# Forming the last outputs of a Strassen-tiled attention layer from sums in PSUM, and reordering the last query projection, scores and output products

## The chip, the core and the metric

The kernel runs on one core of a Trainium2 chip. The metric is device time in microseconds (us): the median of several runs of the whole program. The engines named below are TensorE (PE: matmuls into PSUM), VectorE (DVE: elementwise work), ScalarE (ACT: copies and exponentials), GpSimd (POOL: here it only issues weight loads) and SyncE (SP: here it only issues DMAs).

## The reference

The input `x` is eight sequences of 256 tokens with 512 features. It is normalised to `xn`. Attention with 32 query heads of 128 features and 8 key/value heads (four query heads share one) gives `s`; a gated mixture of small experts gives a factor `g`; the result is `x + s * silu(g)`.

```python
q = (hidden_states @ wq.T).reshape(bsz, q_len, H, HD).transpose(0, 2, 1, 3)
...
scores = scores * scale                       # per-key factors
scores = scores + causal
probs = jax.nn.softmax(scores.astype(jnp.float32), axis=-1).astype(dt)
attn = jnp.einsum('bhqk,bhkd->bhqd', probs, v)
attn = attn.transpose(0, 2, 1, 3).reshape(bsz, q_len, H * HD)
return attn @ wo.T
...
x = x + s * g
```

All data are 32-bit floats.

## The kernel before

**Tiling.** The sequences are worked on in four blocks of two (`tb` 0 to 3; 512 tokens each). Each block has eight groups (`g` 0 to 7), one for each key/value head with its four query heads. A step is one (block, group) pair, 32 in all. A unit is one sequence of one step, so each step has two. A tile name ends in these numbers: unit 7_0 is group 7, first sequence.

**Matrix products.** Every large product (query, key, value and output projection) is cut into 2 x 2 blocks and done with seven block products in place of eight, after Strassen and Winograd. In a query projection (`quad`, line 486) the seven products go to three PSUM banks, `pa`, `pd` and `pe`. Bank `pa` takes four of them one on top of the other; between two of them ScalarE copies the bank aside (`p1`, `u2`, `u3`), and VectorE adds `pd` or `pe` to such a copy to give `cq`. In an output projection (`out_project`, line 841) each of the seven products gets its own bank `po`, and VectorE adds it to one of seven running sums in SBUF, `acc_1` to `acc_7`, which collect over the eight groups. Its left operands are four blocks `a` (the attention outputs, copied from PSUM by ScalarE) and three VectorE sums of them, `s_4` to `s_6`, plus one difference written over an `a`.

**The end of a block.** After group 7, `finish` (line 917) combines `acc_1` to `acc_7` into the four output quarters with seven more additions, and for each quarter multiplies by the stored gate (`g`, half of it), adds `x` (`xf`) and stores it: `result`, line 953.

**A softmax unit** (`softmax`, line 681) has three pieces on TensorE, score rows (7,6), (5,4,3) and (2,1,0) into two rotating PSUM banks `sc`. VectorE scales, masks and takes minima (`z`, `least`). ScalarE takes exponentials into `p`, a single buffer that all units share. VectorE multiplies by the reciprocal sums (`total`) and transposes `p` in 32 x 32 blocks into `blocks`, again a single buffer. SyncE writes `blocks` to DRAM with four DMAs (`there`) and reads it back with one (`pT`). Then `values` (line 806) multiplies it by the value rows (`av`), two pieces for each unit, and ScalarE copies `av` to `a`.

**What sets the order.** TensorE's order is written out by hand: the loop at line 1165 collects the pieces of each step (`sa`, `sb`: scores of the two units; `va`, `vb`: values of the units two back; `oa`, `ob`: output products of the step before and of this one) and lays them down, woven with the next step's query projection (`main`). Step 30 is group 6 of the last block and holds the last query projection; steps 31 to 33 have no projection left to weave. All other engines are ordered by a planner (`Plan.run`, line 195): each job has a due time, derived from the TensorE pieces that need its result, and the planner emits the ready job that is due first. Every engine then runs its queue strictly in that order. Weights for the output products come through a ring of eight buffers (`wo`), for the projections through a ring of nine (`w`); POOL issues a load as soon as the buffer's last reader is done.

In the profile every instruction carries line 118, since all are issued through the `InOrder` helper there; groups are told apart by tile names.

Of the kernel before, what the change touches and what calls it, by code (L numbers as in the profile page):

```python
# [44 lines left out]
P = 128  # L45
# [8 lines left out]
NB = 2  # L54
# [202 lines left out]
def layer(ctx: ExitStack, tc: tile.TileContext, x, wquad, woquad, raT, bT, table, out):  # L257
# [583 lines left out]
    def out_project(tb, g):  # L841
# [19 lines left out]
        for i, (to, a, b, op) in enumerate(Features.steps):  # L861
            a_done[to] = add(
                "dve", 0.61, lambda i=i: sum_up(i),
                after=[a_done[a], a_done[b]] + Features.before(i, a_done),
                opens=[ah[to]] if to != S3 else [], closes=[ah[a], ah[b]],
            )
        pieces = {}

        def product(k, a, w):
# [41 lines left out]
            for i in Outputs.sums:  # L911
                sums_of["wo", g, i].near = (pieces[1], 0.0)
        if g == KV - 1:
            finish(tb)
        return [pieces[k] for k in (1, 2, 6, 5, 7, 4, 3)]

    def finish(tb):
        M = {k: acc[tb, k] for k in range(1, 8)}

        def put(to, a, b, closes=()):  # L920
# [11 lines left out]

        def inputs(b):
            box = {}

            pl, tag = (two, "c") if b and tb == NTB - 1 else (x_pool, "x")
            xh, gh = hold(tag), hold(tag)
            rows = x[bass.ds(tb * TB + b * S, S), :].rearrange("(t p) o -> p t o", p=P)

            def load(what):  # L940
                box[what] = pl.tile([P, 2, D], F32, tag=tag, name=f"{what}{tb}_{b}")
                src = rows if what == "xf" else gates_dram[tb][:, bass.ts(b, 2), :]
                nc.sync.dma_start(out=box[what], in_=src)

            near = (M[2]["last"], -12.0)
            done = [
                add("sp", 0.3, lambda: load("g"), after=gates[tb][2 * b : 2 * b + 2], opens=[xh],
                    near=near, lag=9.0),
                add("sp", 0.3, lambda: load("xf"), opens=[gh], near=near, lag=9.0),
            ]  # L950
            loads[b] = box, [xh, gh], done
# [197 lines left out]
    cleared = add("pool", 2.0, clear)  # L1149

    LAG_V = 2
    held = []

    def part(make, u):
        return make(*units[u]) if 0 <= u < len(units) else []
# [9 lines left out]
    for n in range(len(steps) + 2):  # L1165
        last = n >= len(steps)
        tb, g = (NTB, 0) if last else steps[n]
        (sa, va), (sb, vb) = (
            (part(softmax, u), part(values, u - LAG_V)) for u in (NB * n, NB * n + 1)
        )  # L1170
        ob = out_project(*steps[n - 1]) if 0 < n <= len(steps) else []
        oa, held = held, ob[2:]
        fill = oa[:1] + va[:1] + sa[:1] + oa[1:2] + va[1:] + sa[1:2] + oa[2:4] + sa[2:]
        later = [oa[4:], ob[:1], vb[:1], sb[:1], ob[1:2], vb[1:], sb[1:2], sb[2:]]
        if not last:
            if g == 1 and tb:
                route, turn, silus[tb] = experts(tb)
                fill += route
                later.append(turn)
            at = g if tb == 0 else g - 2  # L1180
            if 0 <= at < NT:
                fill += silus[tb][at]
            if tb + 1 < NTB and g == KV - 2:
                turns = norm(tb + 1)
                for t in range(NT):
                    later[t] = later[t] + [turns[t]]
        later = [piece for some in later for piece in some]
        if n == len(steps) - 1:

            fill, later = sa + sb, oa + va + vb + ob[:2]  # L1190
        main = []
        for q in quads[n + 1] if not last else []:
            main += make_quad(*q)
        if not main:
            lay(fill + later)
        elif len(main) > 7:
            lay(woven(main, fill + later, 0.9))
        else:
            lay(woven(main, fill, 1.0) + later)
# [30 lines left out]
```

## Time and profile before

| what | value |
|---|---|
| median of 3 runs | 1370.39 us (1365.43 to 1372.58) |
| the profiled execution, its own time | 1371.18 us |
| its span, first to last instruction | 1369.4 us |
| TensorE busy | 1334.2 us, 97% |
| VectorE busy | 1096.7 us, 80% |
| ScalarE busy | 618.0 us, 45% |
| mean granted TensorE clock | 0.995 |

A line of the page or of the timeline gives a start (us from the span's start), a duration, the engine, the operation and `output<-inputs`, with how many instructions were merged (`x8`: a 32-bit matmul is two records, so one block product of four matmuls is x8). In square brackets stands the time for which the engine sat idle just before, and what released it. In a table of stretches, each row gives the length of the stretch, then the busy time of each engine in it, the granted TensorE clock, the busy share of the DMA engines and the GB/s moved. The chain of waits is followed back from the last instruction: at each moment it names the work, or the transfer, that the end depended on.

### The profile page before, as it was taken

To read this page: it belongs to the slowest core of one execution; us is meant where nothing else is said; L and a number is where in the kernel's file an instruction comes from. 1 tells how busy PE (TensorE), PEld (TensorE's weight loads), DVE (VectorE), ACT (ScalarE), POOL (GpSimd) and SP (SyncE) were. 2 spreads that over 40 slices of the span, in tenths; PEclk is the share of its full clock that TensorE was granted. 3 is DMA by queue.
4 is the path that set the end of the run, shared out by engine and by line. 5 is a ranking of instruction groups with operands and counts; after the bars stand their busy time and mean duration, and the time that the engine had idled before them with its cause. 6 is when DMAs were issued, how large, how long until landed. Compare 5 with 4: busy or idle time off the path is not lost.

```text
span 1369.4 us, 19896 instructions
## 1 busy us (share of the span) xinstructions
PE 1334.2 (97%) x6512; PEld 1171.1 (86%) x6512; DVE 1096.7 (80%) x2822; ACT 618.0 (45%) x1587; POOL 314.4 (23%) x579
## 2 busy tenths in 40 slices
PE   7999999999999999999999999999999999999986
PEld 6888888888888888888888788888888888888865
DVE  5899989897978759598688776869877878777886
ACT  3465453453534535354434444345543354434430
POOL 2322232222221122222222112222123121221110
PEclk9999999999999999999999999999999999999998
DMA  5578676766766665766766756676667576575563
GB/s 173 187 248 257 204 212 201 233 204 199 236 192 211 200 215 173 218 209 187 219 187 197 217 183 194 190 231 201 173 211 213 168 247 191 179 220 169 185 205 117
DMA packets 106134, 275.81 MB, mean 201 GB/s; under 512 B 15984, under 2 KB 52848, under 8 KB 106032
## 3 DMA queue, kind: packets, MB, share of 16 engines
q0 software_dynamic: 45760, 149.98, 35.5%
q1 hardware_dynamic: 59520, 123.76, 29.2%
q8 instruction: 53, 0.87, 0.3%
q10 hardware_dynamic: 752, 0.80, 0.2%
q14 instruction: 49, 0.40, 0.1%
HBM read 194.79 MB, written 79.69 MB: 200 GB/s over the span
## 4 chain that ended last, share of the span: by engine, by line
PE 83%; DVE 8%; DMA 7%; issue 1%; SPq 0%; ACT 0%; DVEq 0%
PE po L118 24%; PE paq L118 14%; PE av L118 11%; PE sc L118 9%; PE pdq L118 7%; DMA pT<-there 5%; PE pak L118 4%; PE peq L118 3%; PE pav L118 3%; PE pdk L118 2%; DMA there<-blocks 2%; PE pdv L118 1%; DVE blocks L118 1%; PE dle L118 1%; DVE acc L118 1%; PE lme L118 1%
## 5 line engine op out<-in xcount | busy, mean ns | idle before, releaser
L118 ACT ACTIVATE p<-z,least 128x256 f32<-128x256 f32 (+7 forms) x512 | 207.7, 407 | 192.3 <-DVE least L118 138.4
L118 PE MATMUL po<-wo,a 128*128 128x256 f32 x1024 | 241.6, 379 | 1.4 <-ACT a L118 1.4
L118 PEld LDWEIGHTS po<-wo,a 128*128 128x128 f32 x1024 | 192.2, 190 | 25.7 <-ACT a L118 2.2
L118 PE MATMUL av<-pT,v 128*128 128x256 f32 x768 | 186.9, 382 | 10.4 <-DMA pT<-there 10.4
L118 DVE CUSTOM_DVE_ANT_0 z<-sc,tab 128x256 f32<-128x256 f32 (+7 forms) x512 | 134.0, 300 | 68.2 <-PE sc L118 64.8
L118 PE MATMUL po<-wo,s 128*128 128x256 f32 x768 | 183.8, 383 | 3.5 <-DVE s L118 2.7
L118 PE MATMUL paq<-XT,w 128*128 128x256 f32 x768 | 182.0, 380 | 0.3 <-ACT u3q L118 0.3
L118 PEld LDWEIGHTS av<-pT,v 128*128 128x128 f32 x768 | 145.3, 191 | 32.7 <-issue 7.5
L118 PEld LDWEIGHTS sc<-kk,qTq 128*128 128x128 f32 x1024 | 159.3, 191 | 13.4 <-issue 0.8
L118 PE MATMUL sc<-kk,qTq 128*128 128x256 f32 (+7 forms) x1024 | 168.9, 303 | 0.3 <-DVE least L118 0.2
L118 PEld LDWEIGHTS po<-wo,s 128*128 128x128 f32 x768 | 144.7, 191 | 28.2 <-issue 6.3
L118 DVE TENSOR_TENSOR acc<-acc,po 128x512 f32<-128x512 f32 x196 | 132.7, 678 | 41.5 <-PE po L118 40.0
L118 PEld LDWEIGHTS paq<-XT,w 128*128 128x128 f32 x768 | 144.9, 190 | 20.4 <-ACT u2q L118 0.8
L118 POOL DMA_DIRECT2D w<-sums x144 | 78.9, 548 | 347.6 <-PE paq L118 157.1
L118 ACT COPY a<-av 128x512 f32<-128x512 f32 x128 | 74.5, 582 | 181.7 <-PE av L118 181.4
L118 ACT COPY swq<-cq 64x1024 f32<-64x1024 f32 x128 | 133.7, 1045 | 13.7 <-DVE cq L118 9.3
L118 POOL DMA_DIRECT2D w<-in_wquad_dram x148 | 81.0, 548 | 243.8 <-PE paq L118 82.8
L118 DVE STREAM_TRANSPOSE blocks<-p 128x1024 f32<-128x1024 f32 (+1 forms) x128 | 123.4, 967 | 3.3 <-DMA there<-blocks 3.1
L118 DVE TENSOR_SCALAR p<-p,total 128x256 f32<-128x256 f32 (+7 forms) x512 | 116.8, 293 | 2.3
L118 DVE TENSOR_TENSOR qTq<-cq,tab 128x1024 f32<-128x1024 f32 x64 | 78.0, 1219 | 32.2 <-ACT cq L118 32.2
L118 ACT ACTIVATION_READ_ACCUMULATOR p<-z,least 128x1 f32 x512 | 95.8, 187 | 0.0
L118 POOL DMA_DIRECT2D wo<-osums x96 | 52.5, 547 | 153.7 <-PE po L118 153.7
(116 smaller groups left out, 1834.0 us busy)
## 6 DMA issues: line engine op xcount, KB each, us to landing
there<-blocks SPq DMA_DIRECT2D x256, 192.0 KB, 3.7
pT<-there SPq DMA_DIRECT2D x64, 768.0 KB, 5.9
w<-in_wquad_dram POOLq DMA_DIRECT2D x148, 256.0 KB, 4.5
w<-sums POOLq DMA_DIRECT2D x144, 256.0 KB, 4.3
wo<-in_woquad_dram POOLq DMA_DIRECT2D x104, 256.0 KB, 4.9
wo<-osums POOLq DMA_DIRECT2D x96, 256.0 KB, 4.7
sums<-w POOLq DMA_DIRECT2D x48, 256.0 KB, 4.2
osums<-wo POOLq DMA_DIRECT2D x32, 256.0 KB, 4.5
```

Source lines behind the costliest of these rows:

```text
L118: ins = what(*args, **kwargs)
```

## The change

Two things are changed, both for the last token block.

The first is the output products of the last step. `finish` is renamed `put_together` and serves blocks 0 to 2 only; for the last step `out_project` returns `last_products` instead. There the seven running sums are combined after group 6, before the last products are added. The last seven products then go into PSUM in the manner of a query projection: bank `oa` takes A11, S2, S3 and S4's product one on top of the other with ScalarE copies between, `oe` and `od` take one each, and the product S4 x A22 is split in two halves of 128 tokens with a bank each. Each output quarter is one PSUM term (or copy), one prepared sum, the gate and `x`. Quarter (0,1) is gated, added and stored in those two halves as well.

The second is TensorE's order from step 30 on. The scores of step 31 are made in step 30 (`ahead`), and in step 30 the query projection is woven with scores and values alone; the output products that stood between them follow. Step 31 then holds output products and values, and so does the step after it.

```diff
@@ -864,6 +864,8 @@
                 after=[a_done[a], a_done[b]] + Features.before(i, a_done),
                 opens=[ah[to]] if to != S3 else [], closes=[ah[a], ah[b]],
             )
+        if (tb, g) == (NTB - 1, KV - 1):
+            return last_products(n, abox, ah, a_done, wbox, wh, w_done)
         pieces = {}
         def product(k, a, w):
@@ -911,10 +913,151 @@
             for i in Outputs.sums:
                 sums_of["wo", g, i].near = (pieces[1], 0.0)
         if g == KV - 1:
-            finish(tb)
+            put_together(tb)
         return [pieces[k] for k in (1, 2, 6, 5, 7, 4, 3)]
-    def finish(tb):
+    def last_products(n, abox, ah, a_done, wbox, wh, w_done):
+        tb = NTB - 1
+        M = {k: acc[tb, k] for k in range(1, 8)}
+        dve = lambda what, after, **kw: add("dve", 0.61, what, after=after, **kw)
+        turn = []
+        def put(to, a, b):
+            turn[:] = [
+                dve(lambda: nc.vector.tensor_add(M[to]["s"], M[a]["s"], M[b]["s"]),
+                    turn + [M[k]["done"] for k in (to, a, b)])
+            ]
+            M[to]["done"] = turn[0]
+        for to, a, b in ((2, 1, 2), (6, 1, 6), (7, 6, 7), (3, 3, 5), (3, 3, 6), (4, 7, 4), (5, 7, 5)):
+            put(to, a, b)
+        box, loads = {}, {}
+        def load(what, b):
+            pl, tag = (two, "c") if b else (x_pool, "x")
+            rows = x[bass.ds(tb * TB + b * S, S), :].rearrange("(t p) o -> p t o", p=P)
+            def work():
+                box[what, b] = pl.tile([P, 2, D], F32, tag=tag, name=f"{what}{tb}_{b}")
+                src = rows if what == "xf" else gates_dram[tb][:, bass.ts(b, 2), :]
+                nc.sync.dma_start(out=box[what, b], in_=src)
+            after = gates[tb][2 * b : 2 * b + 2] if what == "g" else []
+            loads[what, b] = add("sp", 0.3, work, after=after, opens=[hold(tag)], lag=9.0)
+        for b in range(NB):
+            load("g", b)
+            load("xf", b)
+        def gate(out_, in_, b, f, t=slice(0, 2)):
+            nc.vector.scalar_tensor_tensor(
+                out_, in_, 0.5, box["g", b][:, t, bass.ts(f, 2 * P)], op0=ALU.mult, op1=ALU.mult
+            )
+        def prepare(k, b, f):
+            s = lambda: M[k]["s"]
+            m = dve(lambda: gate(s(), s(), b, f), [M[k]["done"], turn[0], loads["g", b]])
+            M[k]["done"] = dve(
+                lambda: nc.vector.tensor_add(s(), s(), box["xf", b][:, :, bass.ts(f, 2 * P)]),
+                [m, loads["xf", b]],
+            )
+        prepare(4, 1, 0)
+        banks = {}
+        def product(bank, a, w, first, after, opens=(), ts=(0, 1)):
+            def work():
+                if first:
+                    banks[bank] = ps_mm.tile([P, 2, 2 * P], F32, tag="mm", name=f"{bank}{n}")
+                for t in ts:
+                    for h in range(2):
+                        nc.tensor.matmul(
+                            banks[bank][:, t, :], lhsT=abox[a]["a"][:, h, bass.ts(t, P)],
+                            rhs=wbox[w][:, h, :], start=first and t == ts[0] and h == 0,
+                            stop=h == 1, skip_group_check=True,
+                        )
+            return add(
+                "pe", 0.865 * len(ts), work, after=[a_done[a], w_done[w]] + after, opens=opens,
+                closes=[ah[a], wh[w]],
+            )
+        def aside(what, p):
+            def work():
+                box[what] = three.tile([P, 2, 2 * P], F32, tag="side", name=f"{what}{n}")
+                nc.scalar.copy(box[what], banks["oa"])
+            return add("act", 0.5, work, after=[p], opens=[hold("side")])
+        def store(src, b, f, p, after, ts=slice(0, 2)):
+            rows = out[bass.ds(tb * TB + b * S, S), bass.ts(f, 2 * P)].rearrange("(t p) o -> p t o", p=P)
+            return add(
+                "sp", 0.5, lambda: nc.sync.dma_start(out=rows[:, ts], in_=src()), after=after,
+                near=(p, 3.0), lag=4.0,
+            )
+        def bank_and(what, bank, after, closes):
+            return dve(
+                lambda: nc.vector.tensor_add(box[what], box[what], banks[bank]), after,
+                closes=closes,
+            )
+        def result(k, b, f, what, first):
+            s = lambda: M[k]["s"]
+            r = dve(
+                lambda: nc.vector.tensor_add(s(), s(), box[what]), turn + [first, M[k]["done"]]
+            )
+            m = dve(lambda: gate(s(), s(), b, f), [r, loads["g", b]])
+            return dve(
+                lambda: nc.vector.tensor_add(s(), s(), box["xf", b][:, :, bass.ts(f, 2 * P)]),
+                [m, loads["xf", b]],
+            )
+        oa, oe, od, o3, o4 = (hold("mm") for _ in range(5))
+        p1 = product("oa", A11, A11, True, [], [oa])
+        c1 = aside("p1", p1)
+        p2 = product("oe", A12, A21, True, [], [oe])
+        e = bank_and("p1", "oe", [p2, c1], [oe])
+        store(lambda: M[2]["s"], 0, 0, p2, [result(2, 0, 0, "p1", e)])
+        p6 = product("oa", S2, S2, False, [c1])
+        c6 = aside("u2", p6)
+        p5 = product("od", S1, S1, True, [], [od])
+        d = bank_and("u2", "od", [p5, c6], [od])
+        pre = result(3, 0, 1, "u2", d)
+        p7 = product("oa", S3, A12, False, [c6])
+        c7 = aside("u3", p7)
+        d = bank_and("u3", "od", [p5, c7], [od])
+        store(lambda: M[5]["s"], 1, 1, p7, [result(5, 1, 1, "u3", d)])
+        p4 = product("oa", A22, S4, False, [c7])
+        m = dve(
+            lambda: gate(M[7]["s"], banks["oa"], 1, 0), [p4, M[7]["done"], turn[0], loads["g", 1]],
+            closes=[oa],
+        )
+        r = dve(lambda: nc.vector.tensor_add(M[4]["s"], M[4]["s"], M[7]["s"]), [m, M[4]["done"]])
+        store(lambda: M[4]["s"], 1, 0, p4, [r])
+        def half(t, h, after):
+            bank = f"o3_{t}"
+            p = product(bank, S4, A22, True, [after], [h], (t,))
+            m = dve(
+                lambda: gate(M[6]["s"][:, t, :], banks[bank][:, t, :], 0, 1, t),
+                [p, M[6]["done"], turn[0], loads["g", 0]], closes=[h],
+            )
+            r = dve(
+                lambda: nc.vector.tensor_add(M[3]["s"][:, t, :], M[3]["s"][:, t, :], M[6]["s"][:, t, :]),
+                [m, pre],
+            )
+            store(lambda: M[3]["s"][:, t, :], 0, 1, p, [r], t)
+            return p
+        return [p1, p2, p6, p5, p7, half(0, o3, p7), p4, half(1, o4, p4)]
+    def put_together(tb):
         M = {k: acc[tb, k] for k in range(1, 8)}
         def put(to, a, b, closes=()):
@@ -932,13 +1075,11 @@
         def inputs(b):
             box = {}
-
-            pl, tag = (two, "c") if b and tb == NTB - 1 else (x_pool, "x")
-            xh, gh = hold(tag), hold(tag)
+            xh, gh = hold("x"), hold("x")
             rows = x[bass.ds(tb * TB + b * S, S), :].rearrange("(t p) o -> p t o", p=P)
             def load(what):
-                box[what] = pl.tile([P, 2, D], F32, tag=tag, name=f"{what}{tb}_{b}")
+                box[what] = x_pool.tile([P, 2, D], F32, tag="x", name=f"{what}{tb}_{b}")
                 src = rows if what == "xf" else gates_dram[tb][:, bass.ts(b, 2), :]
                 nc.sync.dma_start(out=box[what], in_=src)
@@ -1149,7 +1290,7 @@
     cleared = add("pool", 2.0, clear)
     LAG_V = 2
-    held = []
+    held, ahead = [], {}
     def part(make, u):
         return make(*units[u]) if 0 <= u < len(units) else []
@@ -1165,9 +1306,8 @@
     for n in range(len(steps) + 2):
         last = n >= len(steps)
         tb, g = (NTB, 0) if last else steps[n]
-        (sa, va), (sb, vb) = (
-            (part(softmax, u), part(values, u - LAG_V)) for u in (NB * n, NB * n + 1)
-        )
+        sa, sb = (ahead.pop(u, None) or part(softmax, u) for u in (NB * n, NB * n + 1))
+        va, vb = (part(values, u - LAG_V) for u in (NB * n, NB * n + 1))
         ob = out_project(*steps[n - 1]) if 0 < n <= len(steps) else []
         oa, held = held, ob[2:]
         fill = oa[:1] + va[:1] + sa[:1] + oa[1:2] + va[1:] + sa[1:2] + oa[2:4] + sa[2:]
@@ -1185,12 +1325,19 @@
                 for t in range(NT):
                     later[t] = later[t] + [turns[t]]
         later = [piece for some in later for piece in some]
-        if n == len(steps) - 1:
-
-            fill, later = sa + sb, oa + va + vb + ob[:2]
         main = []
         for q in quads[n + 1] if not last else []:
             main += make_quad(*q)
+        if n == len(steps) - 2:
+            ahead = {u: softmax(*units[u]) for u in (NB * n + 2, NB * n + 3)}
+            a1, b1 = ahead.values()
+            fill = va[:1] + sa + va[1:]
+            later = sb[:1] + oa[:1] + sb[1:] + oa[1:] + a1 + vb + ob[:2] + b1
+        elif n == len(steps) - 1:
+            fill, later = [], oa + va + vb + ob[:2]
+        elif n == len(steps):
+            fill, later = va + vb, oa + ob[:2]
         if not main:
             lay(fill + later)
         elif len(main) > 7:
```

In the compiled order, TensorE's and VectorE's queues are the same up to about 1268 us of the profile before, where the last query projection (`paq_7`) begins; POOL's loads change places from some 20 us earlier. After it TensorE's pieces come in this order (the number of a piece is its group; `sc7_0` stands for all three score pieces of unit 7_0):

```
before: q7 woven with po4 (6,5,7,4), sc6_0, av5_0 | po4_3, po5_1, av5_1, sc6_1, po5_2, po5_4, sc7_0, po5_5,
        sc7_1, po5_6, po5_7, av6_0, po5_3, po6_1, po6_2 | av6_1, po6 (4,5,6,7), av7_0, po6_3, po7_1, po7_2 |
        av7_1, po7 (4,6,5,7,3)
after:  q7 woven with sc6_0, av5_0 | sc6_1, po4 (6,5,7,4,3), sc7_0, av5_1, po5 (1,2,4), sc7_1, po5_5, av6_0,
        po5 (6,7,3) | av6_1, po6 (1,2,6), av7_0, po6 (5,7,4,3) | av7_1, oa, oe, oa, od, oa, o3 half, oa, o3 half
```

## The prediction

> **What bounds the kernel now.** I read the page's busy shares first, then a table of stretches near the end, then TensorE's timeline there, and last the chain of waits.
>
> ```profile
> PE 1334.2 (97%) x6512; PEld 1171.1 (86%) x6512; DVE 1096.7 (80%) x2822; ACT 618.0 (45%) x1587; POOL 314.4 (23%) x579
> ```
>
> ```profile
> 1268.20:1292.00 23.80, 23.80 (x118) 21.17 (x117) 17.50 (x47) 10.19 (x30) 2.19 (x4) 1.00 0.62 199
> 1292.00:1320.00 28.00, 26.96 (x139) 23.51 (x139) 27.62 (x98) 11.48 (x43) 4.40 (x8) 1.00 0.63 196
> 1320.00:1340.00 20.00, 14.84 (x67) 12.13 (x66) 13.04 (x33) 5.06 (x19) 3.30 (x6) 1.00 0.72 218
> 1340.00:1359.30 19.30, 18.44 (x84) 15.28 (x82) 11.03 (x17) 2.35 (x4) 0.00 (x0) 1.00 0.26 84
> 1359.30:1369.40 10.10, 0.00 (x0) 0.00 (x0) 6.62 (x11) 0.00 (x0) 0.00 (x0) 0.65 0.23 78
> ```
>
> The kernel is bound by TensorE, so a change that leaves its instructions alone can win only idle time. That idle time sits at the end. From 1268 to 1292 TensorE is full. From 1292 to 1320 VectorE is full (27.62 of 28). From 1320 to 1340 neither is: TensorE stands for a quarter of the time. After 1359.3 it has nothing left and VectorE works alone.
>
> ```profile
> 1306.21 1.97 PE L118 MATMUL po<-wo,s 128*128 128x256 f32 x8 [0.33 <-PE sc L118]
> ...
> 1325.33 2.83 PE L118 MATMUL av<-pT,v 128*128 128x256 f32 x12 [1.82 <-DMA pT<-there]
> 1328.83 1.99 PE L118 MATMUL po<-wo,a 128*128 128x256 f32 x8 [0.68 <-ACT a L118]
> 1333.49 3.72 PE L118 MATMUL po<-wo,s 128*128 128x256 f32 x16 [2.67 <-DVE s L118]
> ...
> 1350.38 1.99 PE L118 MATMUL po<-wo,a 128*128 128x256 f32 x8 [0.68 <-ACT a L118]
> ...
> 1357.39 1.89 PE L118 MATMUL po<-wo,s 128*128 128x256 f32 x8
> ```
>
> ```profile
> 1325.17 6.37 DMA there<-blocks
> 1331.62 1.25 DVE blocks L118
> 1332.87 0.58 DVE s L118
> ...
> 1341.33 5.41 DMA pT<-there
> ...
> 1358.32 0.70 DVE acc L118
> ...
> 1360.97 4.31 DVE acc L118 x7
> ```
>
> The wait of 2.67 us names the sum `s`, but the chain shows what held it: the transposes of unit 7_1 waited in VectorE's queue for the one `blocks` buffer, which unit 7_0's `there` was still reading, and `s` stood behind them. The tail is eleven VectorE instructions after the last product.
>
> **The change part by part.** TensorE's work from 1268.2 on, by start-to-start times in the timeline: a block product 1.73 us, a unit's scores 0.81 + 0.82 + 0.59 = 2.22, a unit's values 2.59. Left to do are 7 projection products, 4 score units, 6 value units and 5 + 7 + 7 + 7 = 26 output products: 12.1 + 8.9 + 15.5 + 45.0 = 81.5 us. The last product ends at 1357.39 + 1.73 = 1359.1, so 90.9 us passed, 9.4 of them idle. The halved product is the same four matmuls. So there are two gains to size: the 9.4 us, and the 10.3 us from 1359.1 to 1369.4.
>
> *The order (first gain).* The wait chain is: exponentials into the one `p`, scaling, transposes, `there`, `pT`. Scores earlier means transposes earlier, if VectorE can do them. I add up VectorE's new queue with its start-to-start times: minima of a unit 0.63 + 1.23 + 0.43; reciprocal 0.23; scaling 0.84 + 0.92; transposes 1.16 + 0.63; a rope operation 1.13; any 512-wide addition 0.60. The last transpose of each unit then ends:
>
> 5_1 at 1278.4 (before 1277.3). 6_0: ScalarE may start only when `p` is free, 3.4 us of exponentials plus two copies in between take it to 1283.1; then 0.23 + 1.76 + 1.13 + 1.16 + 0.60 + 0.63 on VectorE give 1288.7 (before 1299.9). 6_1: 2.29 minima, 0.23, 1.76, two rope operations 2.26, four additions 2.4, the first two minima of the next unit 1.86 and transposes 1.79 make 12.6, so 1301.3 (1312.8). 7_0: three rope operations 3.4, three additions 1.8, then 0.43, 0.23, 1.76, 1.86 and 1.79 make 11.3, so 1312.6 (1323.1). 7_1: eight additions 4.8, 0.43, 0.23 and 1.76 make 7.2; but the first transpose then waits for 7_0's `there`, which took 8.4 us before (SP from 1323.15 to VectorE at 1331.6), so 1312.6 + 8.4 + 1.16 + 0.60 + 0.63 = 1323.4 (1334.1).
>
> All four come some 11 us earlier. TensorE's new waits follow by laying its queue beside this. Scores of 7_1 want the query's last rope addition at 1306.4, TensorE is there at 1306.1: 0.4. `po5_6` wants `s_5_5` at 1313.8, TensorE is there at 1313.1: 0.8 with the hop. `po5_3` wants a PSUM bank whose addition is queued behind 7_1's reciprocal: 0 or 1.1, depending on which bank it gets; I take 0.5. `av7_1` wants `pT`: 12.8 us passed before from last transpose to `av` (1334.1 to 1346.9), so 1336.2; TensorE arrives at 1268.2 + 81.5 - 14.7 + 1.7 = 1336.7. It is a tie, and on SyncE's queue two loads of 512 KB (`g_1`, `xf_1`) now stand between `there` and `pT` of 7_0 and share the DMA engines with them; I take 1.0. The two ScalarE waits of 0.68 go: after `av7_1` come `oa` and `oe`, whose operands are long there. Small steps 0.3. Sum 3.0 us in place of 9.4: 6.4 gained, TensorE done at 1352.7.
>
> What queues behind the new `oa` bank: each product into it waits for a ScalarE copy of 0.59. Between the two lies a product of 1.73 on another bank (`oe`, `od`) or a half of 0.87, which hides it; without that cover each would be 0.7 us, 2.1 in all. Weights: a `wo` load issues when the product eight places back is done and lands in 4 to 5 us; the nearest pair (`po6_4` to the half using `wo7_2`) lies 13 us apart. Costed at nothing. The seven early additions of sums run while TensorE does `po6` and `av7_1`, where VectorE waited for TensorE before; nothing.
>
> *The tail (second gain).* From `od` on, VectorE does: copy + `od`, into `acc_3`, gate; the second copy + `od`; `acc_3` + `xf`, into `acc_5`, half gate, gate, half addition, `acc_5` + `xf`; the gate of `oa`, half gate, addition, half addition. `od` ends 3 x 1.73 = 5.2 us before TensorE's end. Three operations of 0.60 to 0.72, a wait for the second copy (2.7 before the end), then seven operations at 0.60 and four halves at 0.33 (a 256-wide `z` takes 0.39, start to start 0.32) end about 3.0 us after TensorE. From VectorE's end to the last instruction it was 1369.4 - 1366.0 = 3.4. Tail 6.4 in place of 10.3: 3.9 gained. No row shows a gate read from PSUM; the nearest is `acc<-acc,po` at 679 ns against 688 for `acc<-acc,acc`, so no surcharge. [...] I go by the row.
>
> Sum: 6.4 + 3.9 = 10.3 us. Against the profiled execution, span 1369.4 becomes 1359.1; its own time is 1371.2, 1.8 more, so 1360.9. The median of the runs is 0.8 lower: **1360.1 us**, 0.75% faster. Bounds: `pT` may tie and the bank be free (idle 1.5: 1358.6), or VectorE may be 3 us late at every wait (1363 to 1364).
>
> [...] The row: the longest wait inside is 2.67 us and the granted clock is 1.00 in every stretch until the work ends. [...]
>
> **The rivals.** *VectorE takes the gain (same).* Its queue is full from about 1283 to 1320 in my sum, with no slack; the 1292 to 1320 row shows how that looks. If transposes come only 5 us earlier, `pT` of 7_1 is late by 6 us, idle stays near 9, and only the tail is won: 1370.4 - 3.9 = 1366.5. For: seven waits in my sum are ties. Against: the additions are counted at measured rates, and 1320 to 1340 shows VectorE free for 7 us, which the change fills.
>
> *The wait moves to the last transfer and grows (slower).* `av7_1` is now followed by all seven last products and by the tail, 14.7 + 6.4 us; before, `po7_1` and `po7_2` were done ahead of it. If 7_1's last transpose ends at T, the end is T + 12.8 + 21.1. That equals 1369.4 at T = 1335.5, 12 us later than my 1323.4; slower by over 0.5% from T = 1342, for instance with T = 1344: 1378. It needs VectorE to lose more than the old order did, in spite of the same work.
>
> *The reordering moves nothing (same).* If the planner's order left transposes where they were: 1366 again. The compiled queues speak against it.
>
> **How the numbers follow.** About 0.5% (6.9 us) is what a measurement of this kernel can tell from no change. Forecast of about 1360: 0.74. Gain only in the tail, by either way: 0.20. Last transfer: 0.06. The forecast's own range is 1357 to 1364; reaching to the tail-only case to leave out no more than 2 in 10 at both ends, 1356.5 to 1367. A forecast case above 1363.5 is as likely as a tail-only case below it, so faster 0.73, same 0.21, slower 0.06.
>
> **What would show it.** Right: `blocks` of the last four units end about 11 us earlier; no wait of TensorE over 1.5 us after 1300; ScalarE's waits of 0.68 before the last products gone; VectorE ends about 3 us after TensorE. Wrong: `av` waiting for `pT` over 3 us before the last products; VectorE idle between 1283 and 1312 for `p` or `blocks`; scores waiting for `least` or the rope; the tail longer than 8 us.

## The result and the profile after

The changed kernel takes 1359.0 us (median of 11 timed runs, 1352.75 to 1365.74) against 1371.24 us for the kernel before in the same series (median of 11, 1365.43 to 1372.87). The ratio over all runs of the series is 0.9929, 95% interval 0.991 to 0.9947 (the two medians alone would give 0.9911): 7 to 12 us faster. The whole interval lies outside the 0.5% within which a measurement can't tell it from no change, its near end only just. The forecast was 1360.1 us, 0.75% faster.

The page of the changed kernel has this row of busy shares. Its profiled span is 1356.6 us.

```profile
PE 1330.6 (98%) x6512; PEld 1170.4 (86%) x6512; DVE 1097.6 (81%) x2827; ACT 618.5 (46%) x1590; POOL 314.1 (23%) x579
```

TensorE and its weight loads have the same 6512 instructions as before, and TensorE is still the bound. VectorE has five more.

The two spans differ by 12.8 us, but not all of it is the change. The last query projection begins at 1263.83 us here and at 1268.07 before. TensorE and VectorE run the same queues up to there. Those 4.2 us come mostly from waits of TensorE for `pT` earlier on (8.4 us in all up to 1262 us before, 7.2 here) and from the slow clock that came with them, which differ from one execution to the next. In the profile before, one such wait of 3.35 us, up to 772.70, comes with 6.83 us at half clock, from 771.79 on; in the changed kernel's the same wait is 1.41 us and the clock stays at 1.00. Over all profiles of this study that start lies between 1260.9 and 1273.1. So every profile below is compared from the start of its own last query projection to its end. That stretch is 101.3 us before (one profile) and 92.8 us after, 8.6 less.

The next view is the table of stretches of the changed kernel from that start on. Its columns are the bounds, the length, busy time of TensorE, its weight loads, VectorE, ScalarE and GpSimd with their instructions, the granted TensorE clock, the DMA share and GB/s.

```profile
1263.80:1296.00 32.20, 32.20 (x168) 29.05 (x167) 30.25 (x107) 16.82 (x55) 2.73 (x5) 1.00 0.58 174
1296.00:1322.00 26.00, 25.76 (x125) 22.35 (x123) 25.30 (x68) 9.19 (x37) 4.92 (x9) 1.00 0.91 291
1322.00:1326.00 4.00, 1.88 (x7) 1.49 (x7) 1.50 (x3) 0.00 (x0) 0.56 (x1) 0.84 0.78 277
1326.00:1330.00 4.00, 4.00 (x15) 3.35 (x14) 0.00 (x0) 1.17 (x2) 0.00 (x0) 0.73 0.30 66
1330.00:1350.30 20.30, 20.30 (x95) 17.46 (x93) 16.84 (x27) 2.93 (x5) 1.64 (x3) 1.00 0.24 82
1350.30:1356.60 6.30, 0.10 (x1) 0.00 (x0) 2.91 (x7) 0.00 (x0) 0.00 (x0) 0.91 0.37 125
```

TensorE is now full nearly everywhere, and the tail without it is 6.3 us in place of 10.1. Two rows stand out. From 1322 to 1326 TensorE works less than half the time, and over the two rows from 1322 to 1330 the granted clock falls below 1.00, which it did nowhere inside the work of the stretch before. The DMA engines were 91% busy just ahead of it. TensorE's timeline shows what stopped it (start, length, operation, and in brackets the idle time before it and what ended that):

```profile
1308.92 1.97 PE L118 MATMUL po<-wo,s 128*128 128x256 f32 x8 [0.24 <-PE av L118]
...
1324.22 4.51 PE L118 MATMUL av<-pT,v 128*128 128x256 f32 x12 [2.12 <-DMA pT<-there]
1328.58 1.89 PE L118 MATMUL po<-wo,s 128*128 128x256 f32 x8
...
1335.48 2.75 PE L118 MATMUL av<-pT,v 128*128 128x256 f32 x12
1338.07 1.89 PE L118 MATMUL oa<-wo,a 128*128 128x256 f32 x8
...
1349.38 1.03 PE L118 MATMUL o<-wo,s 128*128 128x256 f32 x4
```

These are all the waits the timeline has left in the changed part: 0.24, and 2.12 at `av7_0` (at 1324.22). That value unit is also slow. Its twelve matmuls take 4.36 us from start to start, and `av7_1` at 1335.48 takes 2.59. `av7_1`, for which the prediction feared, waits for nothing, and neither do the seven products after it.

SyncE's own queue of the changed kernel says why `pT` of unit 7_0 was late (start and length of the issuing instructions):

```profile
1307.67 2.73 SPq L118 DMA_DIRECT2D there<-blocks  x4
1310.44 0.78 SPq L118 DMA_DIRECT2D g<-gates  x1
1311.33 0.78 SPq L118 DMA_DIRECT2D xf<-in_x_dram  x1
1313.14 0.33 SPq L118 DMA_DIRECT2D pT<-there  x1
```

The `pT` issued at 1313.14 landed at 1324.09, 10.95 us later. The prediction's chain has 5.41 for such a transfer of 768 KB. Ahead of it on the queue stand `g_1` and `xf_1`, 1 MB together.

### The profile page after: what moved, and what is told of

Same layout as the page of the kernel before. It is cut to its first block, busy times and chain, and to the rows that moved or that the text cites. A ratio compares the mean times of both kernels' runs of the same rounds, so it can differ in the third digit from the quotient of the medians.

```text
span 1356.6 us, 19913 instructions
## 1 busy us (share of the span) xinstructions
PE 1330.6 (98%) x6512; PEld 1170.4 (86%) x6512; DVE 1097.6 (81%) x2827; ACT 618.5 (46%) x1590; POOL 314.1 (23%) x579
## 4 chain that ended last, share of the span: by engine, by line
PE 83%; DVE 9%; DMA 6%; issue 1%; ACT 1%; SPq 0%; DVEq 0%; ACTq 0%
PE po L118 23%; PE paq L118 14%; PE av L118 10%; PE sc L118 8%; PE pdq L118 7%; PE pak L118 4%; DMA pT<-there 4%; PE pav L118 4%; PE peq L118 3%; PE pdk L118 2%; DMA there<-blocks 2%; PE pdv L118 2%; DVE qTq L118 1%; DVE blocks L118 1%; DVE p L118 1%; DVE acc L118 1%
## 5 line engine op out<-in xcount | busy, mean ns | idle before, releaser
L118 PE MATMUL po<-wo,a 128*128 128x256 f32 x992 | 233.3, 379 | 0.0
L118 PEld LDWEIGHTS po<-wo,a 128*128 128x128 f32 x992 | 186.4, 190 | 22.8
L118 PE MATMUL po<-wo,s 128*128 128x256 f32 x744 | 177.4, 381 | 0.2 <-PE av L118 0.2
L118 DVE TENSOR_TENSOR acc<-acc,po 128x512 f32<-128x512 f32 x189 | 128.2, 679 | 40.5 <-PE po L118 39.1
L118 PEld LDWEIGHTS po<-wo,s 128*128 128x128 f32 x744 | 139.6, 190 | 23.7 <-issue 5.5
L118 POOL DMA_DIRECT2D wo<-in_woquad_dram x104 | 56.9, 548 | 128.4 <-PE po L118 118.5
```

Of the source, the lines that this page charges most:

```text
L118: ins = what(*args, **kwargs)
```

## The experiments

My theory after the result: the order wins the waits for `s` and for the ScalarE copies, the ending wins 4 us of tail, and the two loads give back part of it through the wait of `av7_0` and the slower clock behind it. The rivals: the order alone does everything; the ending alone does half, whatever the order; the wait for `pT` belongs to the earlier transposes and not to the loads.

Each kernel is compared with the kernel before on the same chip. In the table, "stretch" runs from the start of the last query projection to the end. "Idle" is its TensorE part less the 81.5 us of work that the prediction counted, so it holds time lost to a slower clock too.

| kernel | ratio to before (95%) | stretch, us | idle | tail |
|---|---|---|---|---|
| before | 1 | 101.3 | 9.5 | 10.3 |
| changed | 0.9929 (0.991 to 0.9947) | 92.8 | 4.9 | 6.3 |
| changed, second profile | 0.9926 (0.99 to 0.9952) | 92.9 | 5.1 | 6.3 |
| changed, third profile | 0.9926 (0.9904 to 0.9948) | 90.2 | 2.4 | 6.3 |
| order alone | 0.9943 (0.9925 to 0.9961) | 92.8 | 2.1 | 9.2 |
| ending alone | 1.0004 (0.9986 to 1.0022) | 100.6 | 13.5 | 5.6 |
| ending alone, loads late | 0.999 (0.9977 to 1.0003) | 98.8 | 9.4 | 7.9 |
| changed, loads late | 0.9919 (0.9893 to 0.9944) | 88.9 | 0.9 | 6.5 |
| changed, loads doubled | 0.9993 (0.9978 to 1.0008) | 101.0 | 13.3 | 6.2 |
| loads late, GpSimd additions | 0.9909 (0.9885 to 0.9934) | 88.9 | 0.9 | 6.6 |
| before, free buffer for 7_1 | 0.9988 (0.9972 to 1.0005) | 99.5 | 7.7 | 10.3 |

**The changed kernel again.** The same kernel, for a second profile.

> The changed kernel once more, as the measure for the other three on this chip. Ratio to the kernel before 0.9929 as measured, within 0.991 to 0.9947. If the long read-back of the last-but-one unit (10.9 us from issue to landing) belongs to the order and is no accident of one execution, TensorE waits about 2 us for it again, near 56 us after the start of the last query projection.

Measured: 1359.36 us, ratio 0.9926. In this profile `av7_0` waits 2.32 us, and its twelve matmuls are slow again, 4.15 us from start to start.

```profile
1328.75 4.35 PE L118 MATMUL av<-pT,v 128*128 128x256 f32 x12 [2.32 <-DMA pT<-there]
```

So the wait belongs to the kernel and not to one execution, though its length varies (a third profile, below, has 1.29).

**The order alone.** The kernel before with the new loop, and the outputs put together in the old way:

```diff
+        if n == len(steps) - 2:
+            ahead = {u: softmax(*units[u]) for u in (NB * n + 2, NB * n + 3)}
...
         if g == KV - 1:
             finish(tb)
```

> TensorE's new order with the old ending (finish as before, seven output banks). Theory 'two gains that add': only idle time of TensorE goes, the tail stays at about 10.3 us; in the changed kernel idle fell from 9.4 to 4.9 us, so 4.5 us less than before, ratio 0.9967; here the planner puts the gate and input loads elsewhere in SyncE's queue, so up to 8 us less (0.994) if no transfer is late. Rival 'the ending brings it all': no difference, 0.999 to 1.001.

Measured: 1362.0 us, ratio 0.9943. The stretch is 92.8 us, 8.5 less than before. TensorE's timeline of this kernel holds one wait, and its last product is followed by the old, long run of additions:

```profile
1316.05 1.97 PE L118 MATMUL po<-wo,s 128*128 128x256 f32 x8 [1.53 <-issue]
...
1351.53 1.89 PE L118 MATMUL po<-wo,s 128*128 128x256 f32 x8
```

```profile
1315.28 0.67 DVE L118 TENSOR_TENSOR s<-s,a 128x512 f32<-128x512 f32 x1
```

The first view names no releaser for the 1.53 us. It stands at `po5_6`, and TensorE starts 0.10 us after VectorE's `s` of the second view ends, so it is the wait for `s_5_5` that the prediction put at 0.8.

Idle time falls from 9.5 to 2.1: 7.4 us, a little more than the 6.4 that the prediction gave the order. The tail is 9.2, where 10.3 was expected; why it is shorter stays open. This kernel's stretch is as short as the changed kernel's. The timed runs of the same chip put the changed kernel 1.9 us below it (means of 6 and 9 runs, 95% interval about 2.2 to either side), so they don't show that the ending adds anything to the order. No wait for `pT` is left, because the planner puts `g_0`, `xf_0` and `g_1` behind `pT` of unit 6_0 here, and `xf_1` a unit later.

**The ending alone.** The changed kernel with the old loop:

```diff
-        elif n == len(steps) - 1:
-            fill, later = [], oa + va + vb + ob[:2]
-        elif n == len(steps):
-            fill, later = va + vb, oa + ob[:2]
+        if n == len(steps) - 1:
+            fill, later = sa + sb, oa + va + vb + ob[:2]
```

> The new ending with TensorE's old order. Theory 'two gains that add': the tail from TensorE's last product to the end falls from 10.3 to about 6.4 us, idle time stays near 9.4 us: 3.9 us less, ratio 0.9972. Rival 'the ending needs the order' (its early additions need the free VectorE time that the new order makes): 0 to 1 us less, 0.999 to 1.000, with a tail of 9 us or more. Rival 'the ending brings it all': 0.993.

Measured: 1369.02 us, ratio 1.0004: nothing won, although the tail of the profile fell from 10.3 to 5.6. TensorE's timeline of this kernel, three waits and one product without:

```profile
1329.80 4.19 PE L118 MATMUL av<-pT,v 128*128 128x256 f32 x12 [3.69 <-DMA pT<-there]
...
1354.19 3.03 PE L118 MATMUL od<-wo,s 128*128 128x256 f32 x8 [1.99 <-DVE s L118]
1357.01 2.59 PE L118 MATMUL oa<-wo,s 128*128 128x256 f32 x8
1360.27 1.99 PE L118 MATMUL oa<-wo,a 128*128 128x256 f32 x8 [0.68 <-ACT u L118]
```

Idle time has grown from 9.5 to 13.5, and that eats the gain. TensorE waits 3.69 us for a `pT` that is issued behind loads. In the old order `oa` and `oe` stand ahead of `av7_1`, so that `od`, which needs VectorE's sums of the last unit, comes right behind it: 1.99 us. These two stand in place of 1.82 and 2.67 us before, so the waits alone are only some 1.2 us longer. The larger part is the clock: the granted clock is 0.76 over the 7.0 us from 1329 on and 0.75 over the 6.8 from 1352.2 on, so it stood at half for about 3.4 us at each of the two, and the products run slower, `od` in 2.82 from start to start where the changed kernel's took 1.73. And with `od` done before, nothing lies between two products into `oa` while ScalarE copies the bank: 0.68 us, just the 0.7 that the prediction gave as the price without cover. (The kernel before had a ScalarE wait of 0.68 near there too.)

**The ending alone, loads late.** As before this one, with all four loads held until the last `pT` is issued (`gathers` keeps each unit's `pT` transfer):

```diff
             after = gates[tb][2 * b : 2 * b + 2] if what == "g" else []
+            after = after + [gathers[tb, KV - 1, 1]]
```

> The new ending with TensorE's old order, as before, but with the loads of both sequences' gates and inputs issued after the last read-back. Theory 'the ending alone won nothing because its loads came ahead of the read-back of unit 6_1': the wait of 3.7 us there and the half clock after it (1.7 us) go, ratio 0.995 to 0.997. Rival 'the ending needs the order': unchanged, 0.999 to 1.001, with the sums s_7 still late and the old waits in place.

Measured: 1367.82 us, ratio 0.999, not told from before, where 0.995 to 0.997 was expected: the rival held. Two lines of TensorE's timeline of this kernel:

```profile
1349.71 1.99 PE L118 MATMUL od<-wo,s 128*128 128x256 f32 x8 [1.40 <-DVE s L118]
...
1354.11 1.99 PE L118 MATMUL oa<-wo,a 128*128 128x256 f32 x8 [0.68 <-ACT u L118]
```

The wait for `pT` falls from 3.69 to 1.11 us, and the twelve matmuls behind it take 2.83 us in place of 4.19, while a wait for `s` (1.40) and the one for the copy (0.68) stay. The tail is 7.9 us in place of 5.6. The loads now land only 8 to 12 us before TensorE's end, which may be the reason; no run here tests it. So in the old order the ending wins 2.5 us of its stretch in the profile even without the loads in front, not 4. That the new order is needed to cover `od` is read from the 1.40 us here and from no such wait in the changed kernel.

**The changed kernel, second sequence's loads late.** Only `g_1` and `xf_1` are issued behind the last `pT`:

```diff
             after = gates[tb][2 * b : 2 * b + 2] if what == "g" else []
+            after = after + [gathers[tb, KV - 1, 1]] * (b == 1)
```

> The changed kernel with one difference: the loads of the second sequence's gate and input (512 KB each) are issued after the read-back of the last unit, not between the DRAM write and the read-back of the unit before it. Theory 'these two loads make the read-back late': the values of unit 7_0 wait under 0.5 us in place of 2.1, TensorE's clock stays at 1.00 to the end, 3 to 4 us less than the changed kernel: ratio 0.990 to 0.991. Rival 'the DMA engines are full with weights and transfers anyway': the wait stays near 2 us, ratio 0.993 as the changed kernel.

Measured: 1359.02 us, ratio 0.9919, where 0.990 to 0.991 was expected. In the profile the wait of `av7_0` and the slow clock are both gone. Its timeline, and its stretch without TensorE's tail:

```profile
1327.00 2.75 PE L118 MATMUL av<-pT,v 128*128 128x256 f32 x12
```

```profile
1294.90:1351.30 56.40, 56.16 (x270) 49.20 (x269) 49.65 (x120) 13.89 (x45) 8.23 (x15) 1.00 0.68 216
```

TensorE is busy 56.16 of 56.40 us at clock 1.00, and the one wait left is 0.24. The stretch is 88.9 us. The transposes of 7_0 end 43.8 us after the start of the stretch in both kernels, and its `pT` is issued at nearly the same time, 49.3 us in the changed kernel and 49.0 here. What differs is how long the transfer takes to land, here for the changed kernel and then for this one:

```profile
pT<-there SPq DMA_DIRECT2D x1, 768.0 KB, 10.9
pT<-there SPq DMA_DIRECT2D x1, 768.0 KB, 5.9
```

The other two profiles of each have 11.2 and 10.2 us, and 6.6 and 4.2. So the loads are the cause of the wait, and the earlier transposes are not. The tail, 6.5, grows by 0.2 from their later place.

**The changed kernel, those two loads doubled.** Each is made twice, into the same tile:

```diff
                 nc.sync.dma_start(out=box[what, b], in_=src)
+                if b:
+                    nc.sync.dma_start(out=box[what, b], in_=src)
```

> The changed kernel with the loads of the second sequence's gate and input issued twice, in the place they have there. Theory 'the loads ahead of it make the read-back late': 1 MB more at the 270 to 290 GB/s of that stretch is about 3.7 us, so the values of unit 7_0 wait about 6 us in place of 2.1, and a longer half clock may follow: 3.5 to 6 us more than the changed kernel, ratio 0.9955 to 0.9975. Rival 'the engines are full anyway': wait and time as in the changed kernel, 0.993.

Measured: 1368.75 us, ratio 0.9993, where 0.9955 to 0.9975 was expected. The whole gain is gone. TensorE's timeline has 9.83 us of wait where about 6 was expected:

```profile
1331.89 5.21 PE L118 MATMUL av<-pT,v 128*128 128x256 f32 x12 [9.83 <-DMA pT<-there]
```

But this kernel does more than double the bytes. The second load of a pair goes to the tile that the first is still filling, and SyncE's queue waited for the first to land before it issued the second. The first two rows are what that queue waited for between 1307 and 1325 us (total, times, longest). The third has the time that issuing a load of `g` took (least, median and most, in ns). The fourth is the issue of `pT` behind the loads:

```profile
SPq L118 <- DMA xf<-in_x_dram: 6.1, 1, 6.1
SPq L118 <- DMA g<-gates: 5.1, 1, 5.1
L118 SPq DMA_DIRECT2D g<-gates x2: 338/404/471, 1310.1 to 1315.8; - x2
1323.28 0.34 SPq L118 DMA_DIRECT2D pT<-there  x1
```

So `pT` was issued 59.5 us after the start of the stretch in place of 49.3, and landed 8.5 us later. The run shows that what held SyncE's queue ahead of `pT` here, 5.1 and 6.1 us, reached TensorE. How the wait grows with the bytes ahead of it can't be read from it. Behind the wait the twelve matmuls of `av7_0` take 5.05 us from start to start, in place of 2.59.

**Loads late, again, and with GpSimd.** The kernel with late loads once more, and one which also gives the four additions of `xf` to GpSimd to shorten the tail:

```diff
-                lambda: nc.vector.tensor_add(s(), s(), box["xf", b][:, :, bass.ts(f, 2 * P)]),
+                lambda: nc.gpsimd.tensor_add(s(), s(), box["xf", b][:, :, bass.ts(f, 2 * P)]),
```

> The same kernel as in the first series, since its trace showed the wait gone (idle time 0.9 us from the last query projection on, against 4.9) but its median did not differ from the changed kernel's. If the trace is typical, ratio 0.990 to 0.991; if the saved wait comes back elsewhere in most executions, 0.993.

> The kernel with the late loads, and the four additions of the input made on GpSimd in place of VectorE. If VectorE's backlog sets the end (2 us after TensorE's last reads are possible), four additions of 0.6 us less bring VectorE's end 1.5 to 2 us closer to TensorE's: tail about 4.7 us in place of 6.4, ratio about 0.989. If GpSimd's additions slow VectorE's or end later than they, the tail stays at 6 us or grows.

Measured: 1357.96 us, ratio 0.992 (0.9895 to 0.9945), and 1357.72 us, ratio 0.9909. Both stretches are 88.9 us, with tails of 6.5 and 6.6, the second of the two expected cases: the additions moved, and the tail did not. GpSimd's and VectorE's timelines of the second kernel:

```profile
1339.31 2.87 POOL L118 TENSOR_TENSOR acc<-acc,xf 128x512 f32<-128x512 f32 x2 [9.26 <-DVE acc L118]
...
1343.54 1.27 POOL L118 TENSOR_TENSOR acc<-acc,xf 128x512 f32<-128x512 f32 x1 [1.35 <-DVE acc L118]
```

```profile
1340.54 0.69 DVE L118 TENSOR_TENSOR u<-u,od 128x512 f32<-128x512 f32 x1 [0.71 <-PE od L118]
1341.26 1.47 DVE L118 TENSOR_TENSOR acc<-acc,u 128x512 f32<-128x512 f32 x1
...
1344.31 1.05 DVE L118 TENSOR_TENSOR acc<-acc,u 128x512 f32<-128x512 f32 x1
```

An addition costs GpSimd 1.27 us. The VectorE additions that start while it works take 1.47 and 1.05 us in place of 0.69. `u<-u,od`, which reads one operand from PSUM, keeps its 0.69 beside the same GpSimd work. What makes the two longer is not shown. VectorE has four additions less, and still ends 2.83 us after TensorE, against 2.99 in the first kernel with late loads.

**The kernel before, a free buffer for the last transposes.** This tests the reading of the chain before: unit 7_1's transposes go to a slot of `kk` that is free by then, and no longer wait for `blocks`.

```diff
+                if final:
+                    kk = three.tile([P, G, 3, P], F32, tag="kk", name=f"blocks{n}")
+                    box["blocks"] = kk.rearrange("p j i c -> p j (i c)")
```

> The kernel before, with one difference: the transposes of the last unit (7_1) write to a second buffer (a free slot of the key tiles), so they need not wait for the DRAM write of unit 7_0. Reading of the chain before: VectorE's wait of 3.1 us before that transpose goes, and with it TensorE's wait of 2.7 us for the sum s_6_5 queued behind it: 2 to 3 us less, ratio 0.998 to 0.9985. Rival: the sum or its product then waits for something else, or the last read-back lands no earlier and the gain is given back at the values of 7_1: 1.000.

Measured: 1367.49 us, ratio 0.9988, where 0.998 to 0.9985 was expected; it is not told from none. TensorE's timeline of this kernel:

```profile
1335.51 3.72 PE L118 MATMUL po<-wo,s 128*128 128x256 f32 x16 [0.25 <-DVE s L118]
...
1342.36 2.83 PE L118 MATMUL av<-pT,v 128*128 128x256 f32 x12 [1.40 <-DMA pT<-there]
```

The 2.67 us wait for `s` is 0.25 now, so the reading was right: `s` had stood behind transposes that waited for their buffer. But `av7_0` (at 1342.36), which waited for nothing before, then waits 1.40 us for `pT`, and the stretch is only 1.8 us shorter. One wait removed shows the next one. That the order gives 7.4 because it moves the whole line of score, transpose and transfer earlier fits this and the times of the transposes; no run separates them.

**Both again, side by side.** The changed kernel and the one with late loads on one more chip.

> The changed kernel for the third time, beside the next one on the same chip. Ratio to the kernel before 0.991 to 0.9947.

> The late loads for the third time, to tell whether the 4 us that the profiled executions show (idle time 0.9 against 4.9 us) are there in the timed runs too. If so, the median lies 3 to 4 us below the changed kernel's; if the wait is shorter when no profile is taken, 0 to 1.5 us below it, as in the two series so far.

Measured: 1359.31 us, ratio 0.9926 (0.9904 to 0.9948), and 1359.22 us, ratio 0.9917 (0.9891 to 0.9943). In the third profile of the changed kernel `av7_0` waits less, 1.29 us, and its twelve matmuls take 2.67 us from start to start:

```profile
1327.42 2.83 PE L118 MATMUL av<-pT,v 128*128 128x256 f32 x12 [1.29 <-DMA pT<-there]
```

Its stretch is 90.2 us, with late loads 88.9 for the third time. In the profiles late loads are thus worth 1.3 to 4.0 us. In the timed runs, all series together, the changed kernel has a mean of 1359.4 us (23 runs) and the one with late loads 1358.3 (18 runs). The difference of 1.1 us has a 95% interval of about 1.7 to either side, so the timed runs don't settle it. The version with late loads beats the kernel before by 0.8%. That it beats the changed kernel too is shown for this part of the profile only. It does beat the order alone: by 3.5 us on the same chip (6 and 9 runs, about 2.6 to either side).

## Why the prediction was right, and where it was not

**The sum.** Forecast 6.4 us from idle time and 3.9 from the tail, 10.3 in all. The timed runs give 7 to 12 us by their interval, and the three profiles from the start of the last query projection on give 8.6, 8.4 and 11.1. In the first of them 4.6 come from idle time and 4.0 from the tail. That the median of 1359.0 lies 1.1 us from the forecast is in part luck: the first two profiles won about 2 us less in this stretch than forecast, and single executions of the changed kernel lie up to 13 us apart, while the start of the stretch alone varies by 12.

**The scores earlier: right.** The last transposes of the four units were forecast 20.5, 33.1, 44.4 and 55.2 us behind the start of the last query projection. They ended at 20.1, 32.7, 43.8 and 53.2. The first three hold within 0.6 us, so adding up VectorE's queue at start-to-start times worked. The fourth is 2 us early because it no longer waited for 7_0's `there`: VectorE's timeline has no gap before it, and that transfer took 5.5 us (1307.67 to 1313.1) where the prediction carried 8.4 over from before.

**The new idle time: mis-sized and misplaced.** This step failed, and with it one sign of being right, no wait over 1.5 us after 1300. The prediction gave 3.0 us: 0.4 at the scores of 7_1, 0.8 at `po5_6`, 0.5 at `po5_3`, 1.0 at `av7_1` for the loads, 0.3 small. The three profiles have 4.9, 5.1 and 2.4. Of the named waits only `po5_6` showed, with 0.24 (1.53 in the order alone). The loads cost was sought at the wrong unit: the prediction saw `g_1` and `xf_1` between `there` and `pT` of 7_0, but carried their delay on to `av7_1`. The unit whose `pT` stands behind them is 7_0, and `av7_0` waited 2.12, 2.32 and 1.29 us. The late loads show that cause: without the two ahead of it, that `pT` lands 4.2 to 6.6 us after its issue in place of 10.2 to 11.2, and `av7_0` waits for nothing.

**The clock: counted as unchanged, and wrong.** The prediction's sum counts each wait at its length and nothing for the clock; its row has 1.00 in every stretch until the work ends. The 2.67 us wait before had indeed cost no clock. But behind the wait of 2.12 us at `av7_0` the clock stood at 0.50 for 3.41 us, and the twelve matmuls took 4.36 us from start to start in place of 2.59: 1.8 us more on top of the wait. Behind the 2.32 us of the second profile they took 4.15. So the idle time of the first profile is about 2.12 + 1.77 + 0.9, the 0.9 being what the kernel with late loads has too.

The traces of the kernel before and of the changed kernel show a difference between the 2.67 and the 2.12. The clock changes at 771.79, 778.61 and 1362.29 us in the first, and at 1324.75, 1328.16 and 1355.47 in the second; within each, these lie whole multiples of 3.413 us apart. In the rows, with TensorE's busy time, granted clock, DMA share and GB/s, the first three are stretches of that length of the kernel before, cut at such multiples, around the 2.67 us wait, and the last two of the changed kernel, around the 2.12:

```profile
1328.16:1331.57 3.41, 1.99 (x8) 1.00 0.20 70
1331.57:1334.99 3.42, 1.50 (x7) 1.00 0.61 124
1334.99:1338.40 3.41, 3.41 (x18) 1.00 0.95 350
1321.34:1324.75 3.41, 1.29 (x7) 1.00 0.94 334
1324.75:1328.16 3.41, 3.41 (x10) 0.50 0.22 87
```

An edge cut the longer wait in two, and neither stretch had more than 1.92 us of idle time; the shorter wait lay in one stretch whole, 2.12 us. With both traces cut so from their first clock record (17.4 us) to the end, four stretches at full clock have 2.12 us of TensorE idle time or more (2.12, 2.44, 3.01 and 3.41), and half clock follows each; it follows none of those with 1.92 or less. So the one long wait that the prediction had looked at, a spared one, said little; the profile before also has the wait of 3.35 us with its 6.83 us of half clock. An estimate from these numbers: if the place of the edges is chance and the limit lies between 1.92 and 2.12 us, a wait of 2.12 us is caught in four to five of ten executions, since its start must fall in 3.41 - 2.12 = 1.29 us, or in (3.41 - 1.92) + (2.12 - 1.92) = 1.69 us, of every 3.41.

**The tail: right.** Forecast 6.4, measured 6.3. After TensorE's end VectorE worked 2.91 us, forecast 3.0. The gate read from PSUM takes 0.68 us, no more than the gates with both operands in SBUF, whose mean is 686 ns. VectorE's timeline of the changed kernel has it between its neighbours:

```profile
1350.66 0.69 DVE L118 TENSOR_TENSOR acc<-acc,xf 128x512 f32<-128x512 f32 x1
1351.26 0.68 DVE L118 SCALAR_TENSOR_TENSOR acc<-oa,g 128x512 f32<-128x512 f32 x1
1351.86 0.42 DVE L118 SCALAR_TENSOR_TENSOR acc<-o,g 128x256 f32<-128x256 f32 x1
```

So the row's reading, no surcharge, held.

**Gains as independent: only in this order.** The prediction added the two gains. The order alone gave 8.5 us of its stretch and the ending alone 0.7, and together they gave 8.6. The ending takes 2.9 us of tail from what the order leaves (9.2 to 6.3), and its loads give 2.8 us of idle time back (2.1 to 4.9). With the loads late the two together give 12.4. These are the profiles' figures; the timed runs are too coarse to split the gains so.

**The rivals.** VectorE did not take the gain: its transposes came early in all four units. The last transfer did not grow into the bound either: `av7_1` waits for nothing. The rival that the reordering moves nothing falls with the same transposes. That only the tail is won is refuted by the order alone, which is faster with the old ending (0.9943), and by the ending alone, which in the old order gains nothing that the timed runs can tell.

## What to carry to other kernels

When loads are moved or added, read the queue they stand on: a transfer that the bound engine waits for, issued behind 1 MB of loads that nobody needs yet, landed about 5 us later here, and holding the loads back cost only 0.2 us of tail in the new order. Ask of each new wait not only how long it is but what the clock does behind it (2.12 us cost 1.77 more here, and 2.67 us before cost none), and don't take one trace in which a wait was spared for a rule. When an experiment repeats a transfer, look whether the repeat waits for the first. And test two edits apart before adding their gains: here the new ending won nothing in the timed runs without the new order.

## What the runs showed of the hardware

- TensorE ran slower behind waits of 1.99 us (`od`, the ending alone: clock 0.75 over 6.8 us), 2.12 (0.50 for 3.41 us), 2.32 (twelve matmuls of `av` in 4.15 us in place of 2.59), 3.69 (0.76 over 7.0 us) and 9.83 (twelve matmuls in 5.05 us). It did not behind 1.29 us (2.67 us for the twelve), nor behind 1.82 and 2.67 us in the kernel before (clock 1.00). The length alone doesn't decide. In the traces of the kernel before and of the changed kernel the changes of the clock lie whole multiples of 3.413 us apart. Cut at such multiples, the four full-clock stretches with 2.12 us or more of TensorE idle time were each followed by half clock, and none with 1.92 or less was. Inside the work the halved clock came back after a stretch with no idle time, at 778.61 and 1328.16, and not after one with 0.91 us, at 775.20; the two spells lasted 6.83 and 3.41 us. (The trace models the ends of matmuls, so idle times carry a small error.)
- Two loads of 512 KB ahead of a `pT` of 768 KB on SyncE's queue made it land 10.2 to 11.2 us after its issue in place of 4.2 to 6.6, though it was issued at nearly the same time. Whether it waited behind them or shared the engines with them is not shown.
- GpSimd's 128x512 addition took 1.27 us. Two VectorE additions beside it with both operands in SBUF took 1.47 and 1.05 us in place of 0.69, and one that read PSUM kept its 0.69: moving work there did not shorten the tail (6.6 us against 6.5).
